# The second product of the MLP from seven products of quarters in place of eight

## The chip, the cores and the metric

The kernel runs on one core of a Trainium2 chip. The time is device microseconds of that core, median of three runs. Below, TensorE is PE in the profile (its weight loads PEld), VectorE is DVE, ScalarE is ACT, GpSimd is POOL, and SyncE, which sends most transfers, is SP.

## What is computed

64 items, each a float32 matrix x of 256 rows (nodes) by 256 features with its own 256 x 256 adjacency, pass through four layers: attention with four heads, attention with eight heads and an MLP, and two graph attentions. Each layer's result is added to x and normalized.

```python
x = _layernorm(x + _L0_gnn_ref(x, adj, ...))   # four heads of 64
x = _layernorm(x + _L1_gnn_ref(x, adj, ...))   # eight heads of 32, then the MLP
x = _layernorm(x + _L2_gnn_ref(x, adj, W, a))
x = _layernorm(x + _L3_gnn_ref(x, adj, a0, ...))

# within _L1_gnn_ref
    x = x + out                                # out: the attention's
    y = layer_norm(x, gamma2, beta2)
    mlp = jax.nn.gelu(y @ W1 + b1, approximate=False) @ W2 + b2   # 256 -> 1024 -> 256
    return x + mlp
```

## The kernel before

Two items form a group (G = 2), so there are 32 groups, and a group has 512 rows in four blocks of 128. Each group is a generator that yields after each part of its work. ORDER says which group takes the next turn: a digit is an age, the number of groups by which the one that is served is behind the newest. FIRST and LAST do the same for the start and the end. TensorE runs in exactly this order (every matmul is tied to the one before). A framework orders the other engines' instructions.

```python
ORDER = "011225334342343542234235432323132121321132121"

ps_s = ctx.enter_context(tc.tile_pool(name="ps_s", bufs=2, space=bass.MemoryType.PSUM))  # scores
ps_m = ctx.enter_context(tc.tile_pool(name="ps_m", bufs=4, space=bass.MemoryType.PSUM))  # all else ("pm")
...
def scores(i, cs, qT, kT, mask, hd, scale, sums=None):
    ...                                     # matmuls into two tiles ps (layer 1: m = 4 heads)
        for ps in pss:
            e = att.tile([P, 2, QB * N], F32, name="e", bufs=6)
            nc.scalar.activation(e, ps, AF.Exp, scale=scale)
            ...                             # layer 1: mask and row sums, eight instructions for the two tiles
                        nc.vector.scalar_tensor_tensor(e[:, h, k], e[:, h, k], 1.0, mask[:, k], ALU.mult, ALU.mult,
                                                       accum_out=sums[:, kc, c, j:j + 1])

def attention(...):
    for i in range(G):
        for cs in ((0, 1),) if m == 2 else ((0,), (1,)):
            es = scores(i, cs, qT, kT, mask[:, i, :], hd, scale, sums)
            if before:
                products(*before)           # of the turn before: e times v (layer 0) or z (layer 1)
            ...
            yield

def project(dst, srcT, w, extra, row=None, gs=ALL):
    chunks = w.shape[1]                     # 8 for the MLP's second product
    for i in gs:
        pm = ps_m.tile([P, QB, D], F32, name="pm")
        if row is not None:                 # the bias, as a matmul in bf16
            matmul(pm, onesb, row.unsqueeze(1).to_broadcast([P, QB, D]), start=True, stop=False)
        for q in range(QB):
            t = i * QB + q
            for c in range(chunks):
                matmul(pm[:, q, :], srcT[:, c, t * P:(t + 1) * P], w[:, c, :], ...)
            if chunks > NC:
                yield
        o = dst[:, i * QB:(i + 1) * QB, :]
        ...
            nc.vector.tensor_tensor(o, pm, extra[:, i * QB:(i + 1) * QB, 0:D], ALU.add)

def layer1(xb, z, mask):
    zT = transposed(z, gamma1, beta1)
    ...
    yield from attention(zT, zT, z, mask, 32, gamma1, behind)
    yT = transposed(xb, gamma2, beta2)
    yield
    hT = act.tile([P, NF, T], F32, name="hT", bufs=1)
    for f in range(NF):                     # NF = 8
        pm = ps_m.tile([P, T], F32, name="pm")
        for c in range(NC):
            matmul(pm, w1[:, c, f * P:(f + 1) * P], yT[:, c, :], start=c == 0, stop=c == NC - 1)
        nc.scalar.activation(hT[:, f, :], pm, AF.Gelu, bias=b1[:, f:f + 1])
        if f % 2:
            yield
    return x2, hT, both

# group(g), after layers 0 and 1
    def others(gs):
        yield from project(y, hT, w2, both, b2m, gs)
        x = yield from renormed(y, gs)
        x = yield from layer2(x, mask, gs)
        x = yield from layer3(g, x, mask, gs)
```

Names in the profile: the MLP's first product is pm<-xT,L_gnn_W, its second pm<-L_gnn_W,hT; layer 1's scores are ps<-xT, its products of weights and values pm<-e,z; layer 0's are ps<-qT,kT and pm<-e,v; layer 3's scores are ps<-z,xT. Layer 0's result, normalized, is z.

Of the kernel before, what the change touches and what calls it, by code (L numbers as in the profile page):

```python
# [8 lines left out]
F32 = mybir.dt.float32  # L9
# [4 lines left out]
ALU = mybir.AluOpType  # L14
AX = mybir.AxisListType

P = 128
N = 256
D = 256
NC = D // P  # L20
G = 2
QB = N // P
# [4 lines left out]
NF = DFF // P  # L27
# [13 lines left out]
LAST = ("001142322312324311231243212120210102100210100031121201213200120132100101010120100010101102"  # L41
        "01021000001000010010000")
PREPARE = 2


# [355 lines left out]
def usual_input(ctx: ExitStack, tc: tile.TileContext, a: dict, out: bass.AP, flag: bass.AP):  # L401
# [125 lines left out]
    def matmul(*args, **kw):  # L527
        in_order(nc.tensor.matmul(*args, **kw))  # L528
# [151 lines left out]
    def project(dst, srcT, w, extra, row=None, gs=ALL):  # L680


        chunks = w.shape[1]
        for i in gs:
            pm = ps_m.tile([P, QB, D], F32, name="pm")
            if row is not None:
# [4 lines that stand above are left out]
                    matmul(pm[:, q, :], srcT[:, c, t * P:(t + 1) * P], w[:, c, :],  # L691
                           start=c == 0 and row is None, stop=c == chunks - 1 and (row is None or q == QB - 1))
# [3 lines that stand above are left out]
            if extra is None:  # L696
                nc.scalar.copy(o, pm)
            else:
                nc.vector.tensor_tensor(o, pm, extra[:, i * QB:(i + 1) * QB, 0:D], ALU.add)

    def layer0(g, x, mask):
        xT = transposed(x)
# [180 lines left out]
    def group(g):  # L883
        x, adj = load_group(g) if g else first
        yield
        adjb = io.tile([P, TB, N], BF16, name="adjb", bufs=1)
        nc.scalar.activation(adjb, adj, AF.Copy, accum_out=there[:, g:g + 1])
        nc.scalar.activation(adj.bitcast(F32), adj, AF.Square, bias=minus_half, accum_out=edges[:, g:g + 1])
        yield


        pt = io.tile([P, G, QB, N], BF16, name="adjT", bufs=1)
        for t in range(TB):
            i, q = divmod(t, QB)
# [24 lines left out]
        while parts:  # L919
            for r in parts[:turn // QB + 1]:  # L920
                if next(r, END) == END:
                    parts.remove(r)
            turn += 1
            yield

    def prepare():
# [8 lines left out]
        pm = ps_m.tile([P, D], F32, name="pm")  # L935
# [19 lines left out]
        part = setup[:, 3328:3456].bitcast(BF16)  # L955
        for k in range(3):
            nc.vector.tensor_copy(part, left)
            nc.sync.dma_start(b2m[k:k + 1, :], part[0:1, :])
            if k < 2:
                nc.vector.tensor_tensor(left, left, part, ALU.subtract)  # L960

        yield

# [10 lines left out]
        pm = ps_m.tile([P, 2], F32, name="pm")  # L974
# [90 lines left out]
```

## Time and profile before

| | |
|---|---|
| time, median of 3 runs | 2660.74 us (2660.52 to 2662.13) |
| TensorE records: second product of the MLP, 256 wide | 2048, 463.2 us busy |
| TensorE records: bias row, bf16, 512 wide | 64, 24.6 us busy |
| VectorE, sum of two float32 tensors of 512 from PSUM and SBUF (L699) | 691 ns |
| VectorE, product of 1024 float32 elements (L843) | 1217 ns |
| VectorE, sum of 256 float32 elements (L960) | 420 ns |
| ScalarE, copy of 256 elements from PSUM (L853, last group) | 373 ns |
| DMA, mean busy share of the 16 engines | about a tenth |

A float32 matmul leaves two records on TensorE, and each has a weight load. In the timeline a line gives the start and length in us, the engine, the program's line, the operation, out<-in, and in brackets the idle time before it with what ended it. Lengths of matmuls overlap, so the rate is read from starts.

### The profile page before, as it was taken

Reading aid. Unit: us, or ns where it says so; the run is one execution under the profiler, and the core shown is the slowest. Engines: PE = TensorE matmul, PEld = TensorE weight load, DVE = VectorE, ACT = ScalarE, POOL = GpSimd, SP = SyncE. Lnnn points to the kernel's source line nnn. Section 1 sums busy time; section 2 is a strip of 40 time slices with the busy share of each in tenths; the row PEclk is TensorE's granted clock in tenths of the full one; section 3 lists DMA queues with packets and bytes.
Section 4 is the critical chain, followed back from the end, with each engine's and each line's share of the span. In section 5 each row is a group of like instructions: output and inputs, shape, how many; then the busy total and the mean of one; then the engine's idle time right before and its main releaser. Section 6 shows DMA issues by size and latency. Waiting matters only on the chain.

```text
span 2659.6 us, 44925 instructions
## 1 busy us (share of the span) xinstructions
PE 2586.6 (97%) x16648; PEld 1765.4 (66%) x16648; DVE 1967.4 (74%) x6189; ACT 1290.4 (49%) x1995; POOL 586.8 (22%) x1139
## 2 busy tenths in 40 slices
PE   6899999999999999999999999999999999999997
PEld 3467667666667676666676666676676676676665
DVE  4667777777777777777777777777777777777774
ACT  3445544545544445545455444555445455445442
POOL 1112222212222212222222222222222222222121
PEclk8999999999999999999999999999999999999998
DMA  5000011000010100110010110010110001000000
GB/s 155 25 9 29 29 37 30 31 29 29 29 37 28 33 30 26 32 37 26 28 37 25 32 37 25 29 37 21 36 37 25 29 29 29 29 29 17 17 1 25
DMA packets 113729, 83.20 MB, mean 31 GB/s; under 512 B 44256, under 2 KB 113120, under 8 KB 113504
## 3 DMA queue, kind: packets, MB, share of 16 engines
q1 hardware_dynamic: 112144, 79.47, 9.8%
q8 instruction: 134, 2.20, 0.3%
q10 hardware_dynamic: 1360, 0.79, 0.1%
q14 instruction: 91, 0.75, 0.1%
HBM read 54.80 MB, written 17.04 MB: 27 GB/s over the span
## 4 chain that ended last, share of the span: by engine, by line
PE 70%; DVE 17%; POOL 8%; issue 2%; DMA 1%; SPq 1%; ACT 1%; DVEq 0%; POOLq 0%; ACTq 0%
PE pm L528 54%; PE ps L528 10%; PE pm L531 7%; POOL rstd L551 6%; DVE st L544 3%; DVE y L814 2%; DVE y L742 2%; DVE xn L559 2%; POOL ve L547 2%; DVE z L559 2%; DVE mv L545 1%; DVE xb L748 1%; DVE y L741 1%; DVE r L813 1%; POOL ve L549 0%
## 5 line engine op out<-in xcount | busy, mean ns | idle before, releaser
L613 DVE SCALAR_TENSOR_TENSOR e<-e,mask 128x256 f32<-128x256 f32 x1024 | 428.3, 483 | 129.0 <-ACT e L605 129.0
L605 ACT ACTIVATE e<-ps 128x1024 f32<-128x1024 f32 x384 | 372.0, 1019 | 196.6 <-PE ps L528 176.3
L528 PE MATMUL pm<-L_gnn_W,hT 128*128 128x256 f32 x2048 | 463.2, 380 | 0.0
L528 PE MATMUL pm<-xT,L_gnn_W 128*128 128x512 f32 x1024 | 456.4, 594 | 0.0
L528 PEld LDWEIGHTS pm<-L_gnn_W,hT 128*128 128x128 f32 x2048 | 385.3, 191 | 48.9 <-issue 1.1
L786 ACT ACTIVATE hT<-pm,b 128x512 f32<-128x512 f32 x256 | 176.7, 690 | 409.8 <-PE pm L528 409.8
L528 PEld LDWEIGHTS pm<-xT,L_gnn_W 128*128 128x128 f32 x1024 | 193.0, 191 | 204.0 <-issue 199.5
L544 DVE BATCH_NORM_STATS2 st<-y 128x6 f32<-128x256 f32 x768 | 301.1, 408 | 6.7
L551 POOL TENSOR_TENSOR rstd<-ve,mhalf 128x2 f32<-128x2 f32 (+1 forms) x384 | 297.7, 775 | 26.6
L559 DVE TENSOR_SCALAR xn<-y,mv,rstd 128x256 f32<-128x256 f32 x384 | 142.2, 412 | 177.3 <-POOL rstd L551 177.3
L547 POOL TENSOR_SCALAR ve<-mv 128x2 f32<-128x2 f32 x384 | 98.7, 257 | 750.4 <-DVE mv L545 749.9
L772 POOL TENSOR_TENSOR both<-y,xb 128x512 f32<-128x512 f32 x64 | 81.3, 1270 | 757.2 <-DVE y L771 757.2
L607 DVE TENSOR_TENSOR e<-e,mask 128x1024 f32<-128x1024 f32 x128 | 151.0, 1220 | 18.5 <-ACT e L605 18.5
L528 PE MATMUL ps<-xT 32*128 32x256 f32 x2048 | 147.5, 401 | 2.2 <-ACT e L605 1.3
L586 ACT ACTIVATE xT<-pm,beta,gamma 128x512 f32<-128x512 f32 x128 | 92.2, 769 | 108.4 <-PE pm L531 108.3
L528 PE MATMUL pm<-e,z 128*32 128x256 f32 x2048 | 141.5, 385 | 0.4
L528 PEld LDWEIGHTS ps<-xT 32*128 32x128 f32 x2048 | 93.1, 184 | 73.3 <-issue 67.1
L528 PE MATMUL ps<-qT,kT 64*128 64x256 f32 x1024 | 129.2, 392 | 5.2 <-ACT e L605 5.2
L528 PE MATMUL pm<-e,v 128*32 128x256 f32 x2048 | 126.4, 387 | 6.3 <-DVE e L607 6.3
L528 PE MATMUL pm<-L_gnn_WoT,oT 128*128 128x256 f32 x512 | 119.3, 387 | 8.6 <-DVE oT L730 8.6
L528 PE MATMUL pm<-xT,L_gnn_WqT 128*128 128x512 f32 x256 | 121.2, 617 | 3.5 <-ACT xT L584 3.5
L814 DVE SCALAR_TENSOR_TENSOR y<-pm,r,xn 128x256 f32<-128x256 f32 x256 | 120.8, 473 | 2.5
(136 smaller groups left out, 4053.7 us busy)
## 6 DMA issues: line engine op xcount, KB each, us to landing
x<-in_x SPq DMA_DIRECT2D x32, 512.0 KB
adj<-in_adj SPq DMA_DIRECT2D x32, 512.0 KB
rr<-lines SPq DMA_DIRECT2D x128, 128.0 KB
out<-xn SPq DMA_DIRECT2D x31, 512.0 KB
adjT<-adjb SPq DMA_TRANSPOSE x128
L_gnn_W<-in_L_gnn_W SPq DMA_DIRECT2D x2, 1024.0 KB
lines<-zs SPq DMA_DIRECT2D x64, 4.0 KB
out<-xn SPq DMA_DIRECT2D x2, 256.0 KB
```

Source lines behind the costliest of these rows:

```text
L528: in_order(nc.tensor.matmul(*args, **kw))
L531: in_order(nc.tensor.transpose(*args))
L544: nc.vector.bn_stats(st[:, q, :], src[:, t, 0:D])
L547: nc.gpsimd.tensor_scalar(ve[:, 0], mv[:, :, 1], EPS, None, ALU.add)
L551: nc.gpsimd.tensor_tensor(rstd, ve, mhalf[:, 0:k * QB].rearrange("p (k t) -> p k t", k=k), ALU.pow)
L559: nc.vector.tensor_scalar(dst[:, t, 0:D], src[:, t, 0:D], mv[:, q, 0:1], rstd[:, q:q + 1], ALU.subtract, ALU.mult)
L586: nc.scalar.activation(dst[:, c, on], pt[:, on], AF.Identity, bias=bias[:, c:c + 1], scale=scale[:, c:c + 1])
L605: nc.scalar.activation(e, ps, AF.Exp, scale=scale)
L607: nc.vector.tensor_tensor(e, e, mask.unsqueeze(1).to_broadcast([P, 2, QB * N]), ALU.mult)
L613: nc.vector.scalar_tensor_tensor(e[:, h, k], e[:, h, k], 1.0, mask[:, k], ALU.mult, ALU.mult, accum_out=sums[:, kc, c, j:j + 1])
L786: nc.scalar.activation(hT[:, f, :], pm, AF.Gelu, bias=b1[:, f:f + 1])
L814: nc.vector.scalar_tensor_tensor(y[:, t, :], po[:, 0:D], r, x[:, t, 0:D], ALU.mult, ALU.add)
```

## The change

A group's second product is H (512 x 1024, held transposed as hT) times W2 (1024 x 256). Cut both in two each way. The rows of H are cut by item (a11, a12 are the first item's halves over the inner 1024, a21, a22 the second's), W2 into b11, b12, b21, b22 with 512 inner rows and 128 columns each. The plain product has eight products of quarters. By Winograd's form of Strassen's rule seven are enough:

- once, at the start: four differences of W2's quarters (wd)
- per group, on VectorE: s1 = a21 + a22, s2 = s1 - a11, a11 - a21 (written over a21), s4 = a12 - s2
- on TensorE: a11 b11, a22 wd[3], s1 wd[0], s2 wd[1], (a11 - a21) wd[2], a12 b21, s4 b22
- on VectorE: the sums that make the four quarters of the result from these seven, with the residual and bias

Each product has 128 columns instead of 256, and eight matmuls (two row blocks, four chunks). The purpose is less work on TensorE, for more on VectorE. The last group, which is worked item by item, keeps the old product. The three rows of turns are replaced.

```diff
-ORDER = "011225334342343542234235432323132121321132121"
+ORDER = "001222533434324352334422132453233212211231312"
-FIRST = "000000011000002131100110101000000101"
+FIRST = "000000110000021311001001010000001011"
 (LAST likewise: new digits, the same length)
...
+    wd = const.tile([P, 4, NF // 2, P], F32, name="wd")
...
+    def quarters(hT):
+        a = [[hT[:, k * NF // 2:(k + 1) * NF // 2, i * N:(i + 1) * N] for k in range(2)] for i in range(G)]
+        s1 = act.tile([P, NF // 2, N], F32, name="s1", tag="z")
+        s2 = act.tile([P, NF // 2, N], F32, name="s2", tag="kT")
+        s4 = act.tile([P, NF // 2, N], F32, name="s4", tag="qT")
+        nc.vector.tensor_tensor(s1, a[1][0], a[1][1], ALU.add)
+        nc.vector.tensor_tensor(s2, s1, a[0][0], ALU.subtract)
+        nc.vector.tensor_tensor(a[1][0], a[0][0], a[1][0], ALU.subtract)
+        nc.vector.tensor_tensor(s4, a[0][1], s2, ALU.subtract)
+        return a, s1, s2, s4
+
+    def in_seven(dst, of, extra):
+        a, s1, s2, s4 = of
+
+        def product(to, s, w, start=True, stop=True):
+            for q in range(QB):
+                for c in range(NF // 2):
+                    matmul(to[:, q, :], s[:, c, q * P:(q + 1) * P], w[:, c, :], ...)
...
+        pa = ps_m.tile([P, QB, 2, P], F32, name="pm")
+        px = ps_m.tile([P, QB, 2, P], F32, name="pm")
+        product(pa[:, :, 0], a[0][0], quarter(0, 0))
+        w = att.tile([P, QB, P], F32, name="w", bufs=1)
+        nc.scalar.copy(w, pa[:, :, 0])
+        nc.vector.tensor_tensor(r1[:, :, 0], pa[:, :, 0], e1[:, :, 0], ALU.add)
+        matmul(px, onesb, rows, start=True, stop=False)
+        product(px[:, :, 0], a[1][1], wd[:, 3], False, False)
+        yield
+        product(px[:, :, 1], s1, wd[:, 0], False)
+        nc.vector.tensor_tensor(r2, px, e2, ALU.add)
+        nc.vector.tensor_tensor(r1[:, :, 1], px[:, :, 1], e1[:, :, 1], ALU.add)
+        product(pa[:, :, 1], s2, wd[:, 1])
+        nc.vector.tensor_tensor(w, w, pa[:, :, 1], ALU.add)
+        nc.vector.tensor_tensor(r1[:, :, 1], r1[:, :, 1], w, ALU.add)
+        yield
+        product(pa[:, :, 0], a[1][0], wd[:, 2])
+        nc.vector.tensor_tensor(w, w, pa[:, :, 0], ALU.add)
+        nc.vector.tensor_tensor(r2, r2, w.unsqueeze(2).to_broadcast([P, QB, 2, P]), ALU.add)
+        yield
+        py = ps_m.tile([P, QB, 2, P], F32, name="pm")
+        matmul(py[:, :, 0], onesb, rows[:, :, 0], start=True, stop=False)
+        product(py[:, :, 0], a[0][1], quarter(1, 0), False)
+        product(py[:, :, 1], s4, quarter(1, 1))
+        nc.vector.tensor_tensor(r1, r1, py, ALU.add)
+        yield
...
         y, hT, both = yield from layer1(xb, z, mask)
+        of = quarters(hT) if g < B // G - 1 else None
...
-            yield from project(y, hT, w2, both, b2m, gs)
+            if len(gs) == G:
+                yield from in_seven(y, of, both)
+            else:
+                yield from project(y, hT, w2, both, b2m, gs)
...
+        (b11, b12), (b21, b22) = ([w2[:, k * NF // 2:(k + 1) * NF // 2, n * P:(n + 1) * P] for n in range(2)] for k in range(2))
+        for k, (p, m) in enumerate(((b12, b11), (b22, wd[:, 0]), (b22, b12), (b21, wd[:, 1]))):
+            nc.vector.tensor_tensor(wd[:, k], p, m, ALU.subtract)
```

TensorE's order in the middle of the run, as the two programs are built, from the last matmuls of W1 in one group to the fourth e,z of another (x8 and so on are matmuls, two records each):

```
before                                  after
W1 x8                                   W1 x12
transposes xn x8                        transposes xn x8
W1 x4                                   transposes x x8
scores layer 3 x8                       a11 b11 x8, bias, a22 wd[3] x8
bias, second product x8                 transposes z x8
transposes z x8                         scores layer 3 x8
second product x8                       s1 wd[0] x8, s2 wd[1] x8
scores (1) x8                           scores (1) x8
bias, second product x8                 (a11 - a21) wd[2] x8
transposes x x8                         bias, a12 b21 x8, s4 b22 x8
second product x8                       scores (2) x8
scores (2) x8, e,z (1) x8               e,z (1) x8
Wq x4                                   Wq x4
scores (3) x8, e,z (2) x8               scores (3) x8, e,z (2) x8
Wk x4                                   scores (4) x8, e,z (3) x8
scores (4) x8, e,z (3) x8               transposes oT x4
transposes oT x4                        Wk x4
Wv x8                                   Wv x8
scores layer 0 x8, transposes xn x8     e,z (4) x8
e,z (4) x8                              scores layer 0 x8, transposes xn x8
```

Here scores (1) to (4) and e,z (1) to (4) are layer 1's four turns of one group; e,z (n) reads what ScalarE and VectorE made of scores (n).

More of the change, by code (lines that the diff above doesn't have):

```diff
@@ L34 @@
 AT_ONCE = 3
-ORDER = "011225334342343542234235432323132121321132121"
-FIRST = "000000011000002131100110101000000101"
-LAST = ("001142322312324311231243212120210102100210100031121201213200120132100101010120100010101102"
-        "01021000001000010010000")
+ORDER = "001222533434324352334422132453233212211231312"
+FIRST = "000000110000021311001001010000001011"
+LAST = ("011142232321324122331102134212210110012020100031121210213011220010231011000011020010101020"
+        "11012000000100100010000")
 PREPARE = 2
@@ new lines, in in_seven, with quarter, part @@
+    def in_seven(dst, of, extra):
[3 more added lines that the diff above has]
+                for c in range(NF // 2):
+                    matmul(to[:, q, :], s[:, c, q * P:(q + 1) * P], w[:, c, :], start=start and c == 0,
+                           stop=stop and c == NF // 2 - 1 and (start or q == QB - 1))
+        def quarter(k, n):
+            return w2[:, k * NF // 2:(k + 1) * NF // 2, n * P:(n + 1) * P]
+        def part(t, i):
+            return t[:, i * QB:(i + 1) * QB, 0:D].rearrange("p q (n d) -> p q n d", n=2)
+        r1, r2, e1, e2 = part(dst, 0), part(dst, 1), part(extra, 0), part(extra, 1)
+        rows = b2m.rearrange("p (n d) -> p n d", n=2).unsqueeze(1).to_broadcast([P, QB, 2, P])
+        pa = ps_m.tile([P, QB, 2, P], F32, name="pm")
[24 more added lines that the diff above has]
+        yield
@@ L960, in prepare @@
                 nc.vector.tensor_tensor(left, left, part, ALU.subtract)
+        yield
+        (b11, b12), (b21, b22) = ([w2[:, k * NF // 2:(k + 1) * NF // 2, n * P:(n + 1) * P] for n in range(2)] for k in range(2))
+        for k, (p, m) in enumerate(((b12, b11), (b22, wd[:, 0]), (b22, b12), (b21, wd[:, 1]))):
+            nc.vector.tensor_tensor(wd[:, k], p, m, ALU.subtract)
         yield
```

## The prediction

> **What bounds the kernel now.** I read the profile page first: busy time by engine, and the span in 40 slices.
>
> ```profile
> span 2659.6 us, 44925 instructions
> PE 2586.6 (97%) x16648; PEld 1765.4 (66%) x16648; DVE 1967.4 (74%) x6189; ACT 1290.4 (49%) x1995; POOL 586.8 (22%) x1139
> PE   6899999999999999999999999999999999999997
> DVE  4667777777777777777777777777777777777774
> ```
>
> TensorE (PE) is full but for the two ends; VectorE (DVE) comes second, with a quarter of its time free. A table of busy time by stretch then says how full the middle is:
>
> ```profile
> 1200.00:1280.00 80.00, 79.66 (x521) 54.78 (x520) 60.89 (x191) 40.21 (x62) 18.27 (x35) 1.00 0.10 31
> ```
>
> 79.66 of 80 us on TensorE (first pair after the length), 60.89 on VectorE, clock 1.00. The timeline shows the same stage again one group later: the product pm<-v,qT starts at 1314.34 and at 1394.64, so a group costs 80.3 us, and only what shortens TensorE's row within those 80.3 us counts. The one regular hole there is 0.28 us before the z transposes. The stage that the change touches, TensorE's timeline (start, length, count):
>
> ```profile
> 1329.02 2.78 PE L528 MATMUL ps<-z,xT 128*128 128x256 f32 x16
> 1331.64 0.38 PE L528 MATMUL pm<-b2m,onesb 128*128 128x512 bf16 x1
> 1331.85 3.62 PE L528 MATMUL pm<-L_gnn_W,hT 128*128 128x256 f32 x16
> 1335.31 0.38 PE L531 MATMUL pm<-ident,z 128*128 128x128 f32 x2
> 1335.97 1.16 PE L531 MATMUL pm<-ident,z 128*128 128x128 f32 x6 [0.28 <-DVE z L559]
> ```
>
> Starts must be subtracted, since lengths overlap. A float32 matmul is two records. Sixteen records 256 wide go from 1331.85 to 1335.31: 0.216 us each. The x16 above them mixes 8 records 256 wide with 8 that are 128 wide (the list by shape keeps them apart) and takes 2.62 us: (2.62 - 8 x 0.216) / 8 = 0.111 us for a 128-wide record, each with a weight load of its own. Half the width costs 51% of the time, not 50%. The row of biases (bf16, 512 wide) costs 0.21.
>
> [...]
>
> **What the change takes from TensorE.** Per group, removed: 2 items x 2 row blocks x 8 chunks = 32 matmuls, 64 records x 0.216 = 13.82 us, and two bias rows, 0.43. Added: 7 products x 2 x 4 = 56 matmuls, 112 records x 0.111 = 12.43, a bias row of 512 (0.21) and one of 256 (0.11). Net -1.50 us. Only 31 of 32 groups do it; the last keeps the old product. Alone it is 31 x 1.50 = 46 us, 1.7%: even with nothing lost, the 2% line (2607.5) is just missed.
>
> **What it adds elsewhere.** VectorE, per group: four sums over 4 x 256 elements at 1.22 (4.88), five over 256 at 0.42 (2.10), three over 512 at 0.69 (2.07), less the two old additions of 0.69: +7.7 us. ScalarE: one copy of 256 elements, 0.37. At the start four differences of weight quarters, 0.67 each. VectorE goes from 1967 to about 1967 + 31 x 7.7 = 2205 us, 83% of the span. It would not become the bound by its sum; the question is where its queue is late for TensorE, and the rows of turns decide that.
>
> **The new order.** In the built program's order on each engine, a group goes on TensorE: 12 matmuls of W1, transposes of xn and of x, product one, bias, product two, transposes of z, layer 3's scores, products of s1 and s2, layer 1's scores (1), product of the difference, bias, last two products, scores (2), e,z (1), Wq, scores (3), e,z (2), scores (4), e,z (3), oT, Wk, Wv, e,z (4). I walked VectorE and ScalarE through this with the durations above, from the start of those 12 matmuls. VectorE now gathers both rstd waits of z into one, so z comes earlier: last aggregate 11.5, GpSimd's 1.7 us to rstd, then z, xb, z at 0.65 to 0.8 a pair: 15.4. TensorE comes for it at 15.8 (10.3 for W1, 2 x 0.87, 1.78, 0.21, 1.78): the 0.28 goes. After xb (16.3) and 1.2 for the sum, s1 ready 17.5, wanted 19.3; s2 19.0, wanted 21.1; e (1) 30.0, wanted 30.5 (VectorE: four quarter sums to 21.4, then in its order two sums, layer 3's maximum, a sum, two masks, a sum and the next group's adjacency mask to 26.3; ScalarE's 1.25 us on the next adjacency waits for that, so the second exponential ends at 28.6, four masks follow); e (2) 35.7, wanted 36.2. All in time, with half a microsecond to spare.
>
> Not so e (3). The kernel before puts Wk between e,z (2) and scores (4):
>
> ```profile
> 1355.40 1.15 PE L528 MATMUL ps<-xT 32*128 32x256 f32 x16
> 1356.48 1.07 PE L528 MATMUL pm<-e,z 128*32 128x256 f32 x16
> 1357.48 3.70 PE L528 MATMUL pm<-xT,L_gnn_WkT 128*128 128x512 f32 x8
> 1361.11 1.15 PE L528 MATMUL ps<-xT 32*128 32x256 f32 x16
> 1362.18 1.07 PE L528 MATMUL pm<-e,z 128*32 128x256 f32 x16
> ...
> 1356.58 1.94 ACT L605 ACTIVATE e<-ps 128x1024 f32<-128x1024 f32 x2 [0.38 <-PE ps L528]
> ...
> 1357.64 0.42 DVE L613 SCALAR_TENSOR_TENSOR e<-e,mask 128x256 f32<-128x256 f32 x1 [1.21 <-ACT e L605]
> ...
> 1360.06 0.42 DVE L613 SCALAR_TENSOR_TENSOR e<-e,mask 128x256 f32<-128x256 f32 x1
> ```
>
> From the start X of scores (3), 1355.40: exponentials from X+1.2 to X+3.1, eight masks from X+2.2 to X+5.1. With Wk between, e,z (3) came at X+6.8 and found them done. After the change Wk stands behind, and TensorE has only e,z (2) and scores (4) to do, 2.1 us: it would come at X+3.2. Scores (4) also need the two score buffers that the exponentials free at X+2.2 and X+3.1, so they end at X+4.05; the second pair of e,z (3) waits for the seventh mask at X+4.76, and e,z (3) ends at X+5.4 where X+4.16 would have been free. That is +1.25 us a group that VectorE's load has nothing to do with: it is the chain scores, exponential, mask, with too little laid between. Counted as one wait for all eight masks it would be 1.9. Behind it, Wk and Wv (7 us) let VectorE catch up.
>
> **The sum.** Per group: -1.50 (matmuls), -0.28 (z), -0.15 (Wk no longer borders on 32-row matmuls: 3.63 us to such a neighbour against 3.43), +1.3 (e,z (3)), +0.3 for the half-microsecond margins, which will not all hold. That is -0.33, x 31 = -10 us. Start: VectorE stands at the weight differences until W2 has landed (sent behind W1 at 20.8 us; about 28 to 30 by the packets), where before it masked its first e at 28.1; but the second e was only written by 33.9, so I put +1. End: the same kinds of steps in nearly the same order, 0. 2660.7 - 10 + 1 = 2652; since the matmul saving is firm and the margins a guess, 2650.
>
> **Rivals.** (a) The saving comes through whole: 80.3 - 1.93 per group, 60 us, 2601. For it: TensorE is full in 79.66 of 80 us, and someone chose these rows for this program. Against it: the order leaves 2.1 us under a chain of 5.1. (b) VectorE becomes the pace: its idle time is about 19 us a group (80 - 61), and most of it ends with rstd from GpSimd (177 us before xn alone), which a busier queue does not use up unless other work lies between. If two of the four half-microsecond margins break by 0.5 to 1 us each, the group costs 81 to 81.5 and the time 2685 to 2700. For it: added work sits at the fullest place, just behind z. Against it: the new order lays masks between statistics and xn, which saves two waits of 1.1 us. (c) The 128-wide matmuls come slower in long runs, held by weight loads (191 ns each by the page, against 108 of streaming). Against it: eight transposes in a row, each with its load, take 0.87 us, 0.109 each. At 0.125 the saving would be nil, and the time about 2695.
>
> **Range and chances.** With the wait between 1.25 and 1.9 and margins that cost 0 to 0.7, the groups give -21 to +21 us; (a) and the upper half of (b) widen that to 2615 to 2690, eight in ten. Faster by over 2% needs (a) whole: 0.11. Slower by over 2% (over 2714) needs (b) or (c) beyond what I see: 0.06.
>
> **What would show it.** On the page: 16648 + 31 x 48 = 18136 TensorE records, 6189 + 314 = 6503 on VectorE, VectorE near 2205 us busy. In the timeline: 16 records of the new products in 1.78 us (else (c)); no hole before z (else my merged wait is wrong); TensorE waiting 1.2 to 2 us in scores (4) and e,z (3) of every group, released by the exponential and the mask. If that wait is absent or under 0.5, my main step is wrong and (a) holds; if waits stand before the products of s1 and s2 or before e,z (1), it is (b).

## The result: slower, 2726.9 us for 2661.4, and the profile after

The changed kernel takes 2726.91 us (2724.43 to 2727.98), the kernel before in the same session 2661.43 (2660.52 to 2664.07): a ratio of 1.0243, 95% interval 1.0225 to 1.0261. The prediction said 2650, 2615 to 2690.

The profile page after, first lines, to be laid beside those of before:

```profile
span 2726.1 us, 48187 instructions
PE 2612.6 (96%) x18136; PEld 1809.2 (66%) x18136; DVE 2176.0 (80%) x6503; ACT 1307.6 (48%) x2026; POOL 589.9 (22%) x1139
DVE  4678888788788788888888887887887888887884
```

The counts are the predicted ones, 18136 on TensorE and 6503 on VectorE; VectorE is busy 2176 us against 2205 foreseen. TensorE is *busy* for longer than before (2612.6 against 2586.6) although its matmuls are shorter, a first sign that busy time tells little here. The same 80 us stretch in the table of busy time (length, then TensorE, its weight loads, VectorE, ScalarE, GpSimd, then the granted clock):

```profile
1200.00:1280.00 80.00, 78.43 (x552) 54.42 (x553) 67.00 (x198) 38.98 (x60) 16.93 (x32) 1.00 0.11 31
```

TensorE went from 79.66 to 78.43 us: it now has holes. From the start of Wq's first matmul in one group to the next (called the period from here on) it is 82.2 us in most groups against 80.30. Stages are called by the program's tiles: Wq, Wk and Wv are layer 0's projections, q.k its scores (ps<-qT,kT), e,v the products behind them, xn is a normalized x, ex belongs to layer 2, oT is an attention's output transposed; a mask is VectorE's product e<-e,mask. The difference of the two traces, 66.5 us of span, divides so: from the third to the last Wq 60.2 (2387.8 against 2327.6 over 29 groups), before it 4.4, behind it 1.9.

Where the 1.92 us of a period are, by subtracting starts on TensorE's timeline of a steady group, before and after:

| stage on TensorE | before | after | difference |
|---|---|---|---|
| second product with its bias rows | 14.45 | 13.23 | -1.22 |
| z transposes, with the wait ahead of them | 1.65 | 2.83 | +1.18 |
| e,z (2), scores (4), e,z (3) without Wk | 3.08 | 4.71 | +1.63 |
| Wk | 3.63 | 3.44 | -0.19 |
| transposes of x, transposes of ex, W1 | 15.10 | 15.64 | +0.54 |

These sum to +1.94; every other stage is the same to 0.05. TensorE's timeline after, where the products and z are (start, length; in brackets the idle time ahead and what ended it):

```profile
1366.59 1.95 PE L529 MATMUL pm<-wd,hT 128*128 128x128 f32 x16
1368.94 0.56 PE L532 MATMUL pm<-ident,z 128*128 128x128 f32 x2 [0.41 <-DVE z L560]
1370.29 1.09 PE L532 MATMUL pm<-ident,z 128*128 128x128 f32 x6 [0.79 <-DVE z L560]
1371.21 2.78 PE L529 MATMUL ps<-z,xT 128*128 128x256 f32 x16
1373.83 3.74 PE L529 MATMUL pm<-wd,s 128*128 128x128 f32 x32
```

From 1366.59 the sixteen records would be over at 1368.37 (they take 1.78 elsewhere) and z's transposes 0.87 later; layer 3's scores start at 1371.21 instead of 1369.24, so z costs 1.97. And the stretch without Wk:

```profile
1391.02 1.07 PE L529 MATMUL pm<-e,z 128*32 128x256 f32 x16
1392.20 0.70 PE L529 MATMUL ps<-xT 32*128 32x256 f32 x4
1393.12 1.13 PE L529 MATMUL ps<-xT 32*128 32x256 f32 x12 [0.21 <-ACT e L606]
1394.18 1.62 PE L529 MATMUL pm<-e,z 128*32 128x256 f32 x16
```

Scores (4) stop after four records for a buffer that ScalarE's exponentials free, and e,z (3), 1.00 where nothing holds it, takes 1.55. That wait was foreseen. The one at z was not, and it has this behind it on VectorE and GpSimd:

```profile
1365.91 2.35 POOL L777 TENSOR_TENSOR x<-x,beta 128x1024 f32<-128x1024 f32 x1
...
1365.97 2.31 DVE L554 TENSOR_TENSOR rstd<-rstd 128x2 f32<-128x2 f32 x1 [1.66 <-POOL rstd L552]
```

A product of 128x2 numbers takes 2.31 us on VectorE. It starts 0.06 us after GpSimd has begun to add beta to x, and ends with it (1368.28 against 1368.26). The two start together because the addition is next on GpSimd behind the very rstd that VectorE waits for, which ends at 1365.94. In the kernel before the same addition met something else:

```profile
1346.39 2.42 POOL L717 TENSOR_TENSOR x<-x,beta 128x1024 f32<-128x1024 f32 x1 [2.97 <-PE pm L531]
...
1346.53 2.56 DVE L613 SCALAR_TENSOR_TENSOR e<-e,mask 128x256 f32<-128x256 f32 x1
```

There one mask of 0.42 us became 2.56, with no wait of TensorE behind it. The transposes of x, behind which this addition may start, stood late in the group; the new rows put them right ahead of the second product, and the addition lands on the last step of z's statistics.

### The profile page after: what moved, and what is told of

It reads as the page before. It is cut to its first block, busy times and chain, and to the rows that moved or that the text cites. A ratio compares the mean times of both kernels' runs of the same rounds, so it can differ in the third digit from the quotient of the medians.

```text
span 2726.1 us, 48187 instructions
## 1 busy us (share of the span) xinstructions
PE 2612.6 (96%) x18136; PEld 1809.2 (66%) x18136; DVE 2176.0 (80%) x6503; ACT 1307.6 (48%) x2026; POOL 589.9 (22%) x1139
## 4 chain that ended last, share of the span: by engine, by line
PE 47%; DVE 31%; POOL 12%; issue 4%; ACT 3%; DMA 2%; SPq 1%; POOLq 0%; DVEq 0%; ACTq 0%
PE pm L529 31%; PE ps L529 12%; POOL rstd L552 8%; DVE st L545 4%; DVE zs L642 4%; PE pm L532 3%; POOL ve L548 3%; DVE y L874 3%; DVE rstd L554 3%; DVE xn L560 3%; ACT e L606 2%; DVE y L802 2%; DVE qT L901 2%; DVE mv L546 2%; DVE qT L903 1%
## 5 line engine op out<-in xcount | busy, mean ns | idle before, releaser
L614 DVE SCALAR_TENSOR_TENSOR e<-e,mask 128x256 f32<-128x256 f32 x1024 | 363.8, 419 | 70.6 <-ACT e L606 70.5
L560 DVE TENSOR_SCALAR xn<-y,mv,rstd 128x256 f32<-128x256 f32 x384 | 161.3, 467 | 111.3 <-POOL rstd L552 111.3
L832 POOL TENSOR_TENSOR both<-y,xb 128x512 f32<-128x512 f32 x64 | 81.3, 1270 | 694.4 <-DVE y L831 694.4
L529 PE MATMUL ps<-xT 32*128 32x256 f32 x2048 | 171.7, 409 | 11.7 <-ACT e L606 8.3
L529 PE MATMUL pm<-e,z 128*32 128x256 f32 x2048 | 159.3, 388 | 0.3
L529 PEld LDWEIGHTS ps<-xT 32*128 32x128 f32 x2048 | 102.9, 187 | 76.7 <-ACT e L606 42.3
L554 DVE TENSOR_TENSOR rstd<-rstd 128x2 f32<-128x2 f32 x64 | 74.7, 1168 | 97.9 <-POOL rstd L552 97.9
L529 PE MATMUL pm<-L_gnn_W,hT 128*128 128x128 f32 (+1 forms) x1056 | 138.2, 284 | 2.8
L529 PEld LDWEIGHTS pm<-L_gnn_W,hT 128*128 128x128 f32 x1056 | 127.6, 192 | 11.7 <-ACT z L914 9.7
L529 PEld LDWEIGHTS pm<-wd,hT 128*128 128x128 f32 x992 | 117.9, 192 | 11.6 <-DVE w L747 9.3
```

The lines of the kernel that those rows point to most:

```text
L554: nc.vector.tensor_tensor(rstd[:, 0], rstd[:, 0], rstd[:, 1], ALU.mult)
L560: nc.vector.tensor_scalar(dst[:, t, 0:D], src[:, t, 0:D], mv[:, q, 0:1], rstd[:, q:q + 1], ALU.subtract, ALU.mult)
```

## The experiments

The theory after the traces, **A**: the rows of turns lose more than the seven products save; one loss is GpSimd's addition holding VectorE on z's path, the other the Wk turn moved away. The rival, **B**: it is the work added to VectorE that comes late for TensorE, as in rival (b) of the prediction. "L" numbers are lines of each kernel; all times are medians, and the ratios are to the kernel before in the same session.

### The two halves of the change, each alone

Seven products in the rows of the kernel before:

```
 (the changed kernel)
-ORDER = "001222533434324352334422132453233212211231312"
+ORDER = "011225334342343542234235432323132121321132121"
 (FIRST and LAST likewise those of the kernel before)
```

> Seven products, but with the rows of turns of the kernel before. Theory A (the rows of turns are to blame: in the changed kernel's trace the products themselves save about 1.2 us in a period, while z's wait, +1.26 us, and the Wk turn moved behind the e,z (3) turn, +1.62 us, cost more): the period falls below that of before, to 79.0-79.6 us from 80.30, and the time to 2620-2640 us. Rival B (the sums of quarters are to blame: VectorE carries about 6 us more in a period, and its work on z, masks and softmax comes late whatever the rows): period 81.5 us or more, 2700 us or more. Between them, 2645-2690, would say that the old rows put the sums of hT's quarters where TensorE waits for them.

Measured 2910.41 us, ratio 1.0919 (1.0900 to 1.0937), period 88.75. Both theories missed the size; the middle reading, waits at the sums, is the nearest. TensorE's timeline of this run, at the products of s1 and s2:

```profile
1814.71 3.25 PE L529 MATMUL pm<-wd,s 128*128 128x128 f32 x16 [1.16 <-DVE s L709]
1820.38 3.78 PE L529 MATMUL pm<-wd,s 128*128 128x128 f32 x16 [2.42 <-DVE y L739]
```

In these rows no layer 3 scores stand between z and s1, so TensorE comes for s1 before it is made, and for s2's product waits for VectorE's sum y, which stands behind all four sums of quarters. The 32 records take 9.38 us from first start to the next stage, against 3.67; a part of that is a lower clock (granted 0.50 from 1816 to 1824, last section). So some new rows are part of the change: without them seven products can't be used.

Eight products in the rows of the changed kernel:

```
 (the kernel before)
-ORDER = "011225334342343542234235432323132121321132121"
+ORDER = "001222533434324352334422132453233212211231312"
 (FIRST and LAST likewise those of the changed kernel)
```

> The kernel before, eight products and no sums, with the rows of turns of the changed kernel. Theory A (the rows cost): the two waits show here too, so slower than the changed kernel by about the 1.2 us in a period that seven products save: period 83.0-83.6 us, 2745-2770 us. Rival B (the sums on VectorE cost): as the kernel before or quicker, 2640-2670 us.

Measured 2786.66, ratio 1.0478 (1.0444 to 1.0513): a period of 83.65 in 17 groups and 85.3 in eleven. Without one sum of quarters the kernel is slower still, so VectorE's added work isn't what slowed the changed one: B falls. Both waits stand here too: e,z (3) takes 1.55 us, and VectorE's product for rstd is held for as long as in the changed kernel (a line of the list by shape: busy us, mean ns of one, idle time ahead):

```profile
L553 DVE TENSOR_TENSOR rstd<-rstd 128x2 f32<-128x2 f32 x64 | 74.7, 1167 | 97.6 <-POOL rstd L551 97.6
```

With these rows the same, seven products save 83.65 - 82.23 = 1.4 us.

### The wait for z

The changed kernel without the addition (this leaves that work out; beta is zero in these inputs):

```
-        nc.gpsimd.tensor_tensor(x, x, over_blocks(beta0), ALU.add)
```

> The changed kernel without GpSimd's addition of beta to x (2.35 us, 128x1024); that work is left out. Theory A1 (this addition keeps VectorE's 128x2 product for rstd waiting, 2.31 us instead of 0.16, and so delays z): the product takes 0.16 us again, the idle time before z's transposes (0.41 + 0.79 us) goes, the period falls by 1.2 us to about 81.0, the time to 2685-2695 us. Rival B1 (z comes late because VectorE's queue is full of sums): the idle time stays at 0.8 us or more and the time within 10 us of 2727.

Measured 2662.61, ratio 0.9999 (0.9990 to 1.0007), period 80.3: 64 us back, some 25 more than expected, since I had counted the 1.2 us more than before and not the whole 1.97. The wait is gone from TensorE's timeline:

```profile
1334.29 1.04 PE L532 MATMUL pm<-ident,z 128*128 128x128 f32 x8
```

and from the list by shape (busy us, mean ns of one, idle time ahead), first the changed kernel's line, then this run's:

```profile
L554 DVE TENSOR_TENSOR rstd<-rstd 128x2 f32<-128x2 f32 x64 | 74.7, 1168 | 97.9 <-POOL rstd L552 97.9
```

```profile
L554 DVE TENSOR_TENSOR rstd<-rstd 128x2 f32<-128x2 f32 x64 | 10.3, 161 | 97.6 <-POOL rstd L552 97.6
```

Less work might also explain it, so the same work, moved to VectorE:

```
-        nc.gpsimd.tensor_tensor(x, x, over_blocks(beta0), ALU.add)
+        nc.vector.tensor_tensor(x, x, over_blocks(beta0), ALU.add)
```

> The changed kernel with all its work, the addition of beta to x moved from GpSimd to VectorE (one instruction of 128x1024, about 1.2 us, more on VectorE in a period). Theory A1 (it is GpSimd's instruction[...], not the amount of work): the wait for z goes as in the run without the addition, period 80.2-80.6 us, time 2660-2675 us, although VectorE is busier by 1.2 us. Rival B1 (the run without the addition was quicker because there was less to do, or because VectorE's queue is full): z is late by 1.2 us again, period 81.5 us or more, 2700 us or more.

Measured 2687.59, ratio 1.0091 (1.0074 to 1.0108), period 81.0: between the two. The z stage is free (0.87, and the 128x2 product is back at 161 ns), so A1 holds for z. But 0.76 us came in elsewhere: the scores (1) stage takes 1.84 instead of 1.08, because the product wd,hT behind it waits for VectorE's sum w. The addition, 1.22 us there, stands behind the last of the four sums of quarters (which starts at 1434.09) in all groups of the steady part:

```profile
1435.23 1.23 DVE L777 TENSOR_TENSOR x<-x,beta 128x1024 f32<-128x1024 f32 x1
```

The dose doubled (the addition twice: work that the reference does not ask for):

```
         nc.gpsimd.tensor_tensor(x, x, over_blocks(beta0), ALU.add)
+        nc.gpsimd.tensor_tensor(x, x, over_blocks(beta0), ALU.add)
```

> The changed kernel with GpSimd's addition of beta to x done twice, one after the other: 2.35 us of GpSimd's work more in a period than the kernel has. Theory A1 (VectorE's product for rstd is held until GpSimd is done): the time VectorE is held doubles, on one instruction (4.6 us) or on two (2.3 us each), z is 2.35 us later again, period 84.4-84.7 us, 2795-2806 us. Rival B1 (z is late because of VectorE's own queue): no change beyond 0.3 us in a period, below 2740 us.

Measured 2838.11, ratio 1.0659 (1.0640 to 1.0679), period 85.6 to 87.3. VectorE's timeline of this run:

```profile
1763.48 2.31 DVE L554 TENSOR_TENSOR rstd<-rstd 128x2 f32<-128x2 f32 x1 [1.66 <-POOL rstd L552]
...
1765.90 2.76 DVE L560 TENSOR_SCALAR z<-y,mv,rstd 128x256 f32<-128x256 f32 x2
```

The second addition (1765.85, 2.34 us) holds the next instruction that it meets, the scaling of z itself: 2.76 for a pair that takes 0.73. TensorE's idle time ahead of z grew from 0.41 to 2.72, the predicted 2.3; what the period lost beyond that, 1.0 to 2.8 us, is taken up under the hardware below.

In two halves, with the stretch from Wq in the old order (the run of that order alone is under Wk's turn below):

```
-ORDER = "001222533434324352334422132453233212211231312"
+ORDER = "001222533434324352334422132453233212121313212"
 ...
-        nc.gpsimd.tensor_tensor(x, x, over_blocks(beta0), ALU.add)
 ...
             nc.vector.tensor_tensor(y[:, i * QB:(i + 1) * QB, :], pm, over_blocks(bop, QB), ALU.add)
+            nc.gpsimd.tensor_tensor(x[:, i * QB:(i + 1) * QB, :], x[:, i * QB:(i + 1) * QB, :], over_blocks(beta0, QB), ALU.add)
```

> The stretch in the old order, and the addition of beta to x left on GpSimd but in two halves of 128x512, each later, beside the sum that first needs it. Theory A1 (what matters is which VectorE instruction the addition meets, not that it is on GpSimd): z is no longer late, period 78.7-79.4 us, 2612-2635 us. Rival (every GpSimd instruction with such operands costs the path its own time wherever it stands): period 80.0 us or more, 2650 us or more.

Measured 2708.48, ratio 1.0174 (1.0157 to 1.0191), period 81.7, against 81.8 with the addition whole. The edit did not do what it was for: in the built program both halves stand in the old place, as soon as x is transposed. But it shows the hold once more, VectorE's timeline:

```profile
1683.61 1.23 DVE L554 TENSOR_TENSOR rstd<-rstd 128x2 f32<-128x2 f32 x1 [1.66 <-POOL rstd L552]
1684.87 1.19 DVE L555 TENSOR_TENSOR rstd<-rstd,ve 128x2 f32<-128x2 f32 x1
```

Two additions of 1.27 us hold two products, 0.16 us each when free, for 1.2 each.

And the kernel before with its addition on VectorE:

```
-        nc.gpsimd.tensor_tensor(x, x, over_blocks(beta0), ALU.add)
+        nc.vector.tensor_tensor(x, x, over_blocks(beta0), ALU.add)
```

> The kernel before (eight products, its own rows) with the addition of beta to x on VectorE instead of GpSimd. There GpSimd's addition met one mask instruction (2.56 us instead of 0.42) with no wait of TensorE behind it. Theory A (off the path): within 0.3 us of 80.30 in a period, 2650-2670 us. Rival (the held mask cost something after all): 79.5 us or less, below 2640 us.

Measured 2663.61, ratio 1.0000 (0.9991 to 1.0008), period 80.3. There the hold is worth nothing, as theory A said: it met a mask that nobody was waiting for.

### Wk's turn

The changed kernel with two neighbouring turns exchanged, so that Wk stands between e,z (2) and scores (4):

```
-ORDER = "001222533434324352334422132453233212211231312"
+ORDER = "001222533434324352334422132453233212121231312"
```

> The changed kernel with one pair of turns exchanged: Wk's stands again between the e,z (2) turn and the scores (4) turn, as in the kernel before. Theory A2 (without Wk between them, the e,z (3) turn waits for ScalarE's exponentials, 1.62 us in a period): the stretch of scores (4) and e,z (3) takes 4.2-4.4 us instead of 5.78, the period falls by 1.3-1.6 us to 80.6-80.9, the time to 2677-2687 us. Rival B2 (the exponentials are late for a reason of their own, VectorE's or ScalarE's queue): the wait moves to another place of the same stretch and the time stays within 15 us of 2727.

Measured 2711.16, ratio 1.0177 (1.0160 to 1.0194), period 81.8. The stretch fell as said (e,z (2), scores (4) and e,z (3) are 3.08 again, Wk 3.63: 1.43 gained), but 0.99 came back: the second half of q.k 2.54 instead of 1.93, e,v 2.02 instead of 1.75, z 0.1. Neither theory had that. VectorE's, GpSimd's and TensorE's timelines of this run:

```profile
1639.76 1.28 POOL L832 TENSOR_TENSOR both<-y,xb 128x512 f32<-128x512 f32 x1 [13.15 <-DVE y L831]
...
1640.06 2.13 DVE L560 TENSOR_SCALAR xn<-y,mv,rstd 128x256 f32<-128x256 f32 x4
...
1645.87 2.21 PE L529 MATMUL pm<-e,v 128*32 128x256 f32 x32 [0.55 <-DVE e L608]
```

The masks of q.k stand behind four scalings of the norm that follows the MLP. In the kernel before these are two pairs, one 72 us and one 81 us into the period. Here all four come together, 16 us into the next period, and the first takes 1.16 us where 0.41 is usual, beside GpSimd's sum "both". This goes with the rows and not with the seven products: eight products in the changed kernel's rows have the four together at 13.2 us, just as the changed kernel has, and seven in the old rows have two pairs, at 1.6 and 3.7 us. With Wk behind e,z (3), the scalings stood 2.9 us earlier and TensorE came for the masks 1.4 us later, and no wait showed.

The stretch from Wq to the second half of q.k in the old order, e,z (4) included:

```
-ORDER = "001222533434324352334422132453233212211231312"
+ORDER = "001222533434324352334422132453233212121313212"
```

> The changed kernel with the whole stretch from Wq's turn to the second half of q.k in the order of the kernel before: Wk's turn between e,z (2) and scores (4), and e,z (4) behind the transposes of xn and not ahead of the first half of q.k. In the run with Wk's turn alone moved back, the stretch of scores (4) and e,z (3) got its 1.4 us back as expected (3.54 to 2.08), but the second half of q.k took 2.54 us instead of 1.93 and the products e,v after it 2.02 instead of 1.75. Theory A2 (these late masks come of e,z (4) having stood ahead of the q.k turn while ScalarE still owed its exponentials): both times go back to 1.93 and 1.75, period 80.7-81.0 us, time 2680-2690 us. Rival B2 (the exponentials of q.k are late whatever stands ahead of them): period stays at 81.6-82.0, 2705 us or more.

Measured 2712.90, ratio 1.0182 (1.0165 to 1.0199), period 81.8: B2. The wait moved to the transposes of xn (1.57 instead of 1.02) and e,v (2.03); the masks are late whatever stands ahead of them.

### Both mended, and what comes next

The old stretch, and the addition on VectorE:

```
-ORDER = "001222533434324352334422132453233212211231312"
+ORDER = "001222533434324352334422132453233212121313212"
 ...
-        nc.gpsimd.tensor_tensor(x, x, over_blocks(beta0), ALU.add)
+        nc.vector.tensor_tensor(x, x, over_blocks(beta0), ALU.add)
```

> The stretch in the old order and the addition of beta on VectorE, both at once. Theory A (the two losses are separate, and the seven products save what was predicted): period 78.7-79.2 us, 2612-2630 us, quicker than the kernel before by over 1%. Rival (VectorE, 68 us busy in 79, is by then the pace): period 79.8 us or more, 2645 us or more.

Measured 2673.53, ratio 1.0040 (1.0025 to 1.0054), period 80.6: nearer the rival. The late xn and masks remain, and the wait ahead of wd,hT is 0.9.

The transposes of x late again, so that GpSimd's addition follows them at 75 us of the period and not at 62:

```
-ORDER = "001222533434324352334422132453233212211231312"
+ORDER = "001222533434324352334422324532313212211231312"
```

> The changed kernel with one turn moved: the transposes of the next x, and so GpSimd's addition of beta that may follow them, stand some 14 us later, behind the product wd,hT of the third part instead of ahead of the first product of the MLP; nothing else is moved and no work is left out. Theory A1 (the addition costs only because it meets VectorE's 128x2 products for rstd of z): these take 0.16 us again, the 1.95 us before and in z's transposes go, period 80.2-80.8 us, 2662-2682 us. Rival B1 (the addition costs its time wherever it stands[...]): period 81.7 us or more, 2708 us or more.

Measured 2685.36, ratio 1.0084 (1.0066 to 1.0102), period 80.9, just above A1's range: 42 us back for one turn moved, with all the work done and GpSimd's addition as long as before. The mean of the 128x2 product is 194 ns. The gain is 1.3 us in a period and not 1.97, because without the transposes of x ahead of them z's come 1.1 us earlier and find z not ready.

With Wk's turn in the old place as well:

```
-ORDER = "001222533434324352334422324532313212211231312"
+ORDER = "001222533434324352334422324532313212121231312"
```

> The run before with Wk's turn between e,z (2) and scores (4) as well. Wk's turn moved alone gave 0.44 us in a period (1.43 at scores (4) and e,z (3), of which 0.99 was lost again at q.k, e,v and z). Expected, if the two do not meet: the same 0.4 or a little more, period 79.7-80.4 us, 2645-2668 us. If the x transposes and their addition now delay the masks of the first scores, 80.6 us or more.

Measured 2672.30, ratio 1.0039 (1.0024 to 1.0054), period 80.5, just above the range: the two gains add up (0.4), from a start that was higher than expected. What is left at z:

```profile
1659.42 1.09 PE L532 MATMUL pm<-ident,z 128*128 128x128 f32 x6 [0.73 <-DVE z L560]
```

The addition on VectorE in two halves, behind the last sum of quarters, with Wk's turn in the old place (the changed kernel again, its other rows kept):

```
-ORDER = "001222533434324352334422132453233212211231312"
+ORDER = "001222533434324352334422132453233212121231312"
 ...
-        nc.gpsimd.tensor_tensor(x, x, over_blocks(beta0), ALU.add)
 ...
             nc.vector.tensor_tensor(y[:, i * QB:(i + 1) * QB, :], pm, over_blocks(bop, QB), ALU.add)
+            nc.vector.tensor_tensor(x[:, i * QB:(i + 1) * QB, :], x[:, i * QB:(i + 1) * QB, :], over_blocks(beta0, QB), ALU.add)
```

> The changed kernel with Wk's turn between e,z (2) and scores (4), and the addition of beta to x on VectorE in two halves of 128x512 behind the last sum of quarters (they stood ahead of the second sum in the run with the addition on VectorE, which then showed a wait of 0.75 us before the third part's product wd,hT). Theory A (the waits add up: z's 1.95 goes, Wk's turn gives 0.44, and behind the sums the addition delays no product): period 79.7-80.0 us, 2640-2655 us, quicker than the kernel before. Rival (any 1.3 us more on VectorE in this stretch delays a product or a mask by about as much): period 80.4 us or more, 2665 us or more.

Measured 2675.04, ratio 1.0040 (1.0026 to 1.0054), period 80.7: the rival. z is free, but TensorE waits further on:

```profile
1671.52 2.05 PE L529 MATMUL pm<-wd,hT 128*128 128x128 f32 x16 [0.89 <-DVE w L747]
```

VectorE has no idle time from 1661.73 (z) to that sum w at 1671.04: z and xb, four sums of quarters, two halves of the addition, three sums of products, layer 3's maximum. The expectation had the addition's place in the earlier run wrong: there too, and in the run of both mended, it stood behind the last sum of quarters. So this run repeats that place, and whether another place in the row would cost less is not shown.

That run with the norm behind the MLP and e,z (4) in the old order too:

```
-ORDER = "001222533434324352334422132453233212121231312"
+ORDER = "001222533434324352334422132453233212132113212"
```

> The run before, and the stretch from Wq to the second half of q.k wholly in the order of the kernel before: e,z (4) behind the first half of q.k, and the layer norm behind the MLP ahead of the scores (4) turn. VectorE's four instructions for that norm (0.41 us each, the first 1.16 while GpSimd adds) then stand ahead of the masks of e,z (2) and not between those and the masks of q.k. Theory A2 (it is these four instructions that made the masks of q.k late): xn's transposes, q.k and e,v take 1.02, 1.93 and 1.75 us again, period 78.8-79.3 us, 2612-2632 us. Rival B2 (ahead of the masks of e,z (2) they make those late instead, waiting for GpSimd's rstd): a wait of about 1 us at e,z (2), period 79.7 us or more.

Measured 2714.95, ratio 1.0188 (1.0171 to 1.0205), period 82.0. Both halves of the expectation came true: q.k, xn and e,v are 1.93, 1.02 and 1.75 again (A2), and e,z (2) takes 3.06 instead of 1.00 (B2). The four scalings wait for GpSimd's rstd at the head of VectorE's queue (two of them behind 1.14 us of idle time), and the masks behind them wait too.

Last layer's scores ahead of z's transposes, in the rows with x late and Wk between:

```
-ORDER = "001222533434324352334422324532313212121231312"
+ORDER = "001222533434324352334422342532313212121231312"
```

> Seven products, the x transposes late, Wk's turn between e,z (2) and scores (4), and the last layer's scores (2.62 us of products that do not need z) ahead of z's transposes instead of behind them. Theory (z is ready at 61.7 and 63.2 us of the period, and only TensorE's order made it wait): the wait of 1.03 us goes, period 79.3-79.6 us, 2630-2645 us, quicker than the kernel before by 0.7 to 1.2%. Rival (the scores, earlier on VectorE, delay z or the sums of quarters by as much): period 80.2 us or more, 2660 us or more.

Measured 2711.94, ratio 1.0183 (1.0169 to 1.0197), period 81.3 in most groups and 82.9 in ten: the rival, and by more. z is no longer waited for; the product of the third part is:

```profile
1693.43 2.05 PE L529 MATMUL pm<-wd,hT 128*128 128x128 f32 x16 [1.89 <-DVE w L747]
```

With the scores earlier, layer 3's maximum and its two masks (0.95 and 1.02 us) come ahead of that sum.

Eight products in these rows:

```
 (the kernel before)
-ORDER = "011225334342343542234235432323132121321132121"
+ORDER = "001222533434324352334422342532313212121231312"
 (FIRST and LAST those of the changed kernel)
```

> The kernel before, eight products without sums, in the rows of that run. Theory A (seven products save 1.5 us in a period whatever the rows, as they did in the changed kernel's rows, 83.7 against 82.2): period 80.8-81.2 us, 2678-2695 us. Rival (the rows alone make the gain): 79.7 us or less, 2645 us or less.

Measured 2679.95, ratio 1.0059 (1.0043 to 1.0074), period 80.7: inside the theory's time, a little under its period, and still against it, for its point was that seven save 1.5 us whatever the rows. Here seven take 0.55 us longer than eight, or 2.2 in the ten groups: 1.92 more ahead of the third part's product, against 1.32 saved at the matmuls. The late masks of q.k are not among the difference, for eight products have them as well (q.k's second half 2.59, e,v 2.02), behind the same four scalings:

```profile
1373.53 2.13 DVE L559 TENSOR_SCALAR xn<-y,mv,rstd 128x256 f32<-128x256 f32 x4
```

Two of the four sums left out (the products take other operands of the same size, so this is not the reference's result):

```
-        nc.vector.tensor_tensor(s2, s1, a[0][0], ALU.subtract)
-        nc.vector.tensor_tensor(s4, a[0][1], s2, ALU.subtract)
-        return a, s1, s2, s4
+        return a, s1, s1, s1
```

> The run with the last layer's scores ahead of z's transposes, without two of the four sums of quarters (the second and fourth, 2.4 us of VectorE's work; the products take other operands of the same size in their place): this leaves out part of the computation, TensorE's work is the same. Theory (VectorE's chain from z to the sum that frees the third part's product is the pace of this stretch): the scores (1) turn before that product takes 1.08 us again instead of 3.04, period 79.3-79.6 us, 2630-2645 us. Rival (a buffer, or ScalarE): the wait stays, period 81 us or more, 2700 us or more.

Measured 2651.14, ratio 0.9948 (0.9932 to 0.9965), period 79.8. The wait falls from 1.89 to 0.38:

```profile
1653.86 2.05 PE L529 MATMUL pm<-wd,hT 128*128 128x128 f32 x16 [0.38 <-DVE w L743]
```

So in these rows it is VectorE's row of work between z and w that TensorE waits for, as the theory had it; 0.45 us more than expected is left. No kernel with seven products that does all the work beat the kernel before; the nearest is 2672.30 (x late, Wk between).

## Why the prediction was wrong

Step by step, per group.

**-1.50 for the matmuls: right in kind,** 0.28 too large. Sixteen records take 1.78 us, so rival (c) is out, but 1.88 where the neighbour is of another kind: between the two kernels 1.22 shows.

**-0.28, "z comes earlier: ... 15.4 ... the 0.28 goes": this step failed,** and with it the prediction. z became +1.18, a miss of 1.46 us x 31 = 45 us. The walk had VectorE's product for rstd at its usual 0.16 us and left GpSimd's other work out; the runs show that product held for 2.31 us by the addition of beta, and TensorE's stage of z 1.97 us longer for it. With the addition away, z's transposes run without any wait, but with less to spare than the walk had: the two rstd waits of z are not one, they stand one behind the other (1.39 and 1.66 us), and in the run without the addition z is complete 16.3 us after the start of W1's 12 matmuls and not 15.4, while TensorE comes at 16.2 and needs only the first half then. The prediction named the sign ("no hole before z (else my merged wait is wrong)"), but gave the wrong reason for it in advance: the hole is the addition's. What was missed lay open in the profile of before: the group list has an addition of 128x1024 on GpSimd, the timeline a mask of 2.56 us beside it, and the order of the built program says that the transposes of x, behind which it starts, move by 15 us. The runs show the hold as long as the addition beside it: 2.31 us beside 2.35, 1.23 and 1.19 beside 1.27.

**+1.3 at e,z (3): right in mechanism,** 0.3 small: 1.63 measured, between the two ways in which it had been counted (1.25 and 1.9). It was the main step of the prediction and cannot be had back by undoing it, which I hadn't seen: Wk between gives 1.43 and loses 0.99.

**-0.15 for Wk:** 0.19. **+0.3 for margins:** no wait showed at s1, s2 or e,z (1). In their place stand 0.54 us at borders between stages (x transposes 1.13 for 0.87, ex 0.67 for 0.49, W1 0.10), which I had not counted.

**Start +1, end 0:** 4.4 and 1.9. I didn't follow these up.

The sum with z right, -1.50 + 1.18 - 0.15 + 1.3 + 0.3, would be +1.13 a group, about 2697; with the other terms as measured it is the 2727.

**Rival (b)** named a time nearer the result for a reason that the runs reject for the changed kernel: with no added VectorE work at all the same rows are slower, not faster. It is true of the versions beyond it. Once z is free, VectorE's row from z to w is what TensorE meets in most of them (0.76 to 1.9 us), and each order tried put the wait somewhere else. That is where the saving of the seven products goes: they ask VectorE for four sums in the one stretch where it also makes z. The four scalings ahead of q.k's masks come with the new rows, whichever the product.

## What to carry to other kernels

Ahead of a change of order, list what each large GpSimd instruction will run beside afterwards: here a 128x2 VectorE instruction took 2.31 us beside a 128x1024 GpSimd one of 2.35, and whether the hold cost anything depended on what it met (without the addition the changed kernel got 64 us back; in the kernel before, where it held a mask, moving it gave a ratio of 1.0000). Work saved on a full TensorE can be lost to what is added to another engine, if that falls in the stretch where that engine is already at the path: in the rows with the scores first, 1.32 us saved at the matmuls stood against 1.92 more ahead of one of them. Count that engine's work between two points of the path, not over the span. And try a new algorithm and a new order apart: here each alone has a longer period (88.75 us for seven products in the old rows, 83.65 for eight in the new) than both together (82.2), so what the seven products are worth depends on the rows.

## What was not expected of the hardware

Not only the 128x2 product and the mask were held: a scaling of one tensor (TENSOR_SCALAR) took 1.16 us instead of 0.41 beside GpSimd's sum "both" of 1.28 us, and 2.44 at most beside the second addition of 2.34. A BATCH_NORM_STATS that ran beside the same sum "both" took 0.43, where its mean is 0.41.

A wait of 1.86 us cost more than its length. The table of busy time of the run with the scores first, two stretches behind the same wait in two groups (1.86 us and 1.84); the number after the engines is the granted clock:

```profile
1530.00:1532.00 2.00, 2.00 (x11) 2.00 (x11) 1.97 (x11) 1.71 (x3) 0.00 (x0) 0.50 0.01 4
```

```profile
1613.00:1615.00 2.00, 2.00 (x21) 1.99 (x20) 2.00 (x12) 1.80 (x3) 0.00 (x0) 1.00 0.00 0
```

In one group TensorE ran at half clock after it (16 records in 3.34 us for 1.89), in the other not; this is the 1.6 us between the two periods of that run. What sets the groups apart in this trace is when the wait falls. Every change of its granted clock stands on a grid of 3.41 us, and in the steady part the clock is halved ten times, for one step of the grid each (its mean is 0.985, against 0.990 in the changed kernel). The step ahead of each of these ten holds 1.82 us or more of TensorE's idle time, nearly the whole wait; no other step holds over 1.75. The same two waits by steps of the grid (TensorE's idle time is the length less the first number behind it):

```profile
1526.04:1529.45 3.41, 1.55 (x20) 1.01 (x19) 3.41 (x8) 1.02 (x1) 0.00 (x0) 1.00 0.00 0
1529.45:1532.87 3.42, 3.42 (x18) 3.42 (x18) 2.64 (x12) 2.58 (x4) 0.00 (x0) 0.50 0.07 15
```

```profile
1607.96:1611.37 3.41, 2.27 (x27) 1.73 (x26) 3.41 (x6) 1.02 (x1) 0.00 (x0) 1.00 0.00 0
```

No threshold follows: in the changed kernel, between 155 and 2600 us, the clock was halved twice, from 711.5 and from 1865.2 for 3.41 us each, and the steps ahead held 1.60 and 1.53 us of idle time; no other step there held over 1.21. The same half clock stands in the run with the addition twice (0.50 from 1770 to 1772, behind 2.72 us of idle) and in the one with the old rows, where it lasts from 1816 to 1824. Two groups of the changed kernel take 84.2 and 84.3 us for 82.2; these two steps of half clock are theirs, both behind the wait for z.
